# W3 product with features in partitions, its result turned by exchange and block turn, and one written list for the last two groups

## The chip, the cores and the metric

The kernel runs on one core of a Trainium2 chip. TensorE does the matmuls, VectorE and ScalarE move and combine what TensorE leaves in PSUM, GpSimd (POOL in the profile) does the small arithmetic of the norms and issues some DMAs, and SyncE (SP) issues the other DMAs. The metric is the time of one execution on the device in microseconds. The kernel before took 2526.16 us (median of 3 runs, 2524.74 to 2527.15).

## What is computed

The input x is [128, 128, 256] in fp32: 128 graphs of 128 nodes with 256 features; adj is one 128 x 128 matrix for all graphs. Four layers follow each other, and each adds its result to x after a layer norm and a relu. Cut to what matters here:

```
x += relu(gated messages along adj, along adj.T, and the node itself)   # layer 0
x += softmax(q k.T / 16, causal) v, then Wo                             # layer 1
x += A (relu(A (relu(A (h W1)) W2)) W3)     # layer 2: 256 -> 512 -> 1024 -> 256
x += BN(relu(BN(A_hat h W1.T)) W2.T)        # layer 3: 256 -> 512 -> 256
```

A mixes the nodes of one graph. The batch norms of layer 3 take mean and variance over all 16384 rows, so everything behind the first of them waits until all graphs have come to it. The change concerns the product by W3 in layer 2.

## The kernel before, in words

**Groups and streams.** The graphs are worked on in 32 groups of 4 (G), 512 tokens (T) each. The first pass brings every group through layers 0, 1 and 2 and through layer 3 up to its first product, which is stored as Z; it also stores x as X3. Between the passes the statistics of the first batch norm are closed (bn_affine, L1064), while 41 transposes keep TensorE running (awake, L1061). The second pass (L1151 on) normalizes Z, multiplies by the second matrix and keeps the statistics of the second batch norm; at the end the results are normalized, transposed and added to X3.

**Order of the work.** Each layer of a group is a Python generator that hands over after each small step. In turn g of the first pass (loop at L1041) four are in progress: A is layer 0 of group g+2, B layer 1 of group g+2 (its start belongs to the turn before, where it is called b), C layer 2 of group g, D layer 3 of group g-1 (its start, d, likewise). The string TURN (L983) says whose step is next, and in_turn (L88) pins the instructions of each step behind those of the step before on PE, VectorE, ScalarE, POOL and SP. So each engine's order is that of the list, and an instruction that waits holds up all that come later on its engine. HEAD (L1015) is the list for the start and group 0. The last turn, g = 31, follows FINAL (L992) by longer stages that are not pinned.

**Products.** `seven` (L524) multiplies two matrices as 2 x 2 blocks with seven block products: p_x, p_y, p_z are its PSUM tiles, `kept` (L529) copies one to SBUF on ScalarE (tiles ..._t), and `put` adds or copies to the result. Who is stationary and who moves is set by the product function. rows_by_half (L492) holds activations stationary, 128 tokens at a time, and streams 128 columns of weights (the matmul is at L499): the result has tokens in partitions. columns_by_half (L507) holds 128 columns of weights and streams 256 tokens (L516): the result has features in partitions. W2's product and layer 3's use the second form, W1's and W3's the first.

**Layer 2 before.** layer2 (L851) makes h2T, the 1024 features after W2, with features in partitions. The sums of its quarters are h2s. The third product multiplies h2s by the block combinations SETS["3"] of W3 with rows_by_half (L897), 7 x 8 matmuls of 128 columns per group, and put_s (L884) writes s with tokens in partitions: three additions on VectorE (L892) and one copy on ScalarE (L890), 128x256 each. Then pr = A s (L905, two matmuls of 512 columns; its stationary operand s must have tokens in partitions), VectorE adds pr to x (L907), and POOL stores x as X3 (L911). s shares its buffer, tag "qv", with layer 1's qv.

**Transposition by exchange.** Where other tiles have to be turned, the kernel uses swap and cut: swap (L439) stores a tile to DRAM with four DMAs (L444) and loads it back with one (L448), all on SP, so that blocks of 32 x 32 change their places; cut (L450) turns each block within itself with one VectorE transpose (L452). Layer 1 does this for h (DMAs hc, cut into hT, 128x1024) and for the attention weights (pc, cut into p, 128x512), layer 0 for the gate matrix (cc, cut into m). p's cut is what the attention product py (L794) waits for.

**Layer 3.** layer3 (L914) norms x, mixes it into gT (pg, L926, evicted at L466), makes its sums gs, and multiplies with columns_by_half (pz). VectorE and ScalarE bring pz to zo (L938, L946), bn_stats (L942, L952) records the statistics, and SP stores zo in two halves as Z (L957). bn_part (L973) aggregates the statistics with one bn_aggr for each of four feature chunks: "most1" for groups 0 to 29, ahead of the last turn in the program (L1045), "last1" for groups 30 and 31 after it (L1060). Names in the profile: mv_most and mv_last.

Of the kernel before, what the change touches and what calls it, by code (L numbers as in the profile page):

```python
# [15 lines left out]
P = 128  # L16
# [6 lines left out]
def kernel(  # L23
# [468 lines left out]
    def rows_by_half(a_r, b_r, wide):  # L492


        def product(r, pb, first):
            nk = a_r[r].shape[1]
            for rr in range(2):
                for c in range(nk):
                    nc.tensor.matmul(  # L499
                        pb[:, rr, :], a_r[r][:, c, rr * P : (rr + 1) * P], b_r[r][:, c, :wide],  # L500
                        start=(first and rr == 0 and c == 0), stop=(c == nk - 1),
                        skip_group_check=True,
                    )

        return product
# [344 lines left out]

    def layer2(g):  # L851

        xt, us = X[g], US[g]
        h2T = w.tile([P, HC2, T], FP, tag="h2T", name=f"h2T_{g}", bufs=1)

        a11, a12, a21, a22 = quarters_t(h2T)
        ex = w.tile([P, 3, HC2 // 2, T // 2], FP, tag="h2s", name=f"h2s_{g}", bufs=1)
        h2s = (a11, a12, ex[:, 2], a22, ex[:, 0], ex[:, 1], a21)

        def wide(q):  # L860
            def put(ij, pb, other):
                i, j = ij
                j = j * HC2 // 2 + 2 * q
                dst = h2T[:, j : j + 2, i * T // 2 : (i + 1) * T // 2]
                if other is None:
                    nc.scalar.activation(dst, pb, AF.Relu)
                    mine = slice(2 * q, 2 * q + 2)
                    yield SPLIT
                    yield from sums(
                        nc.vector,  # L870
                        [a[:, mine] for a in (a11, a12, a21, a22)], ex[:, :, mine],
                    )
                else:
                    nc.vector.tensor_tensor(dst, pb, other, ALU.add)  # L874
                    yield SPLIT
                    nc.scalar.activation(dst, dst, AF.Relu)  # L876

            return seven(
                columns_by_half(us, SETS["2"], 2 * q), put, [P, 2, T // 2], f"p2_{g}_{q}"
            )  # L880

        S = []

        def put_s(ij, pb, other):  # L884
            i, j = ij
            if not S:
                S.append(w.tile([P, G, D], FP, tag="qv", name=f"s_{g}", bufs=1))
            dst = S[0][:, 2 * i : 2 * i + 2, j * P : (j + 1) * P]
            if other is None:
                nc.scalar.copy(dst, pb)  # L890
            else:
                nc.vector.tensor_tensor(dst, pb, other, ALU.add)  # L892
            return ()

        yield from wide(0)
        late = wide(1)
        third = seven(rows_by_half(h2s, SETS["3"], P), put_s, [P, 2, P], f"p3_{g}")  # L897
        if g == LAST:
            for part in (late,) * 6 + (third,):
                yield from stage(part)  # L900
        yield from late
        yield from third
        for q in range(G // 2):
            pr = bank([P, 2, D], f"pr_{g}_{q}")
            nc.tensor.matmul(pr, a2T, S[0][:, 2 * q : 2 * q + 2, :], start=True, stop=True)  # L905
            yield SPLIT
            nc.vector.tensor_tensor(  # L907
                xt[:, 2 * q : 2 * q + 2, :], pr, xt[:, 2 * q : 2 * q + 2, :], ALU.add
            )
            yield SPLIT  # L910
        nc.gpsimd.dma_start(X3[g].rearrange("(b n) d -> n b d", n=P), xt)  # L911
        yield

    def layer3(g):  # L914


        parts = [ALL] if g < LAST else HALVES
        for bs in parts:
            relus = yield from norm(g, 3, bs)
            if g < LAST:  # L920
                yield
            h = yield from relus()
            yield
        gT = tile_of(g, parts[0], [P, DC, T], "dT", f"gT_{g}", 2)
        for i, bs in enumerate(parts):
            yield from mixed(gT, h, ahT, f"pg_{g}_{i}", (nc.vector.tensor_copy,), bs)  # L926
            if g < LAST:
                ex = w.tile([P, 3, 1, T // 2], FP, tag="ex", name=f"gs_{g}", bufs=2)
                gs = yield from sums(nc.vector, quarters_t(gT), ex)
            yield  # L930
        z = ZT[g] = [zp.tile([P, 2, T], FP, tag="z", name=f"zo_{g}_{j}") for j in range(2)]
        done = []

        def put(ij, pb, other):
            i, j = ij
            dst = z[j][:, :, i * T // 2 : (i + 1) * T // 2]
            if other is not None:
                nc.vector.tensor_tensor(dst, pb, other, ALU.add)  # L938
            if g >= LAST - 1:
                at = 2 * g - LAST + 1 + i  # L940
                for jj in range(2):
                    nc.vector.bn_stats(  # L942
                        stats1[:, 2 * j + jj, at, :], (pb if other is None else dst)[:, jj, :]
                    )
            if other is None:
                nc.scalar.copy(dst, pb)  # L946
            done.append(j)
            if done.count(j) == 2:
                if g < LAST - 1:
                    for jj in range(2):  # L950
                        yield SPLIT
                        nc.vector.bn_stats(stats1[:, 2 * j + jj, g, :], z[j][:, jj, :])  # L952

        if g < LAST:
            yield from seven(columns_by_half(gs, SETS["b"], 0), put, [P, 2, T // 2], f"pz_{g}")
            for j in (1, 0):
                nc.sync.dma_start(Z[g][:, 2 * j : 2 * j + 2, :], z[j])  # L957
            yield
            return
        for i, j in (0, 0), (1, 0), (0, 1), (1, 1):  # L960
            pb = bank([P, 2, T // 2], f"pz_{g}_{i}_{j}")
            for jj in range(2):
                for c in range(DC):
                    at = (2 * j + jj) * P
                    b = bw1T_12[:, jj * P : (jj + 1) * P] if (c, j) == (0, 1) else bw1T[:, c, at : at + P]
                    nc.tensor.matmul(
                        pb[:, jj, :], b, gT[:, c, i * T // 2 : (i + 1) * T // 2],
                        start=(jj == 0 and c == 0), stop=(c == DC - 1), skip_group_check=True,
                    )
            yield from put((i, j), pb, None)  # L970
            yield

    def bn_part(stats, nch, groups, name):  # L973

        mv = const.tile([P, nch, 2], FP, name=f"mv_{name}")
        for j in range(nch):
            nc.vector.bn_aggr(mv[:, j, :], stats[:, j, groups].rearrange("p g s -> p (g s)"))
        return mv[:, :, 0], mv[:, :, 1]
# [2 lines left out]


    TURN = (  # L983
        "DCDCCCCCBDBBBBBBBBABBBDDDAABBBBCCDDAAAABBDCCCBBCCBBACCAADDDDAADDAAACCDBA"
        "CCCCCCCCCCCCDDDABCCCCCCBBBADDBBBCCBBBBCCDCCACCCCCCAAAAABBbbbBBBBBDDBBBCC"
        "CCCbCCbBBBBBBBBBDDBBBBBBCDBDDBCCCdBBBBCCCdBBdBBBBBbB"
    )
    BEGUN = 6
    PINNED = tuple(
        getattr(mybir.EngineType, e) for e in ("PE", "DVE", "Activation", "Pool", "SP")  # L990
    )
    FINAL = "CCCCCCCCDCCCCCCCCCCDCCCCDDdDDddDdDdDDdddd"  # L992
    US = {}
    AHEAD = 3

    def stage(stream):

        for end in stream:
            if not end:
                yield  # L1000
                return
            yield end
# [6 lines left out]
    def part(f, g):  # L1009
# [8 lines left out]
        "dbbbeddbedfffoobbbbbbpppdopdbbbbbbbbdCfffffdddfAAffnCCfffffffffAddddfofp"  # L1018
        "ofoAddddndpAAfffddddddddfdffddCddfCCCCCCffnnACCCCfCoAACCAACCACCCCCCCCCCA"
        "AnnnnnAfCCCCCCoffffffAffffCCCCCCACCACCCCfffnCfAAAAABBBffffffffnCConBfBff"  # L1020
        "ffoofCCCfCffffooCCfffCCCCCDDDfffffffffffffB"
    )
    load_x(AHEAD)
    ds, bs = layer3(0), layer1(2)
# [13 lines left out]
        for _ in stream[k]:  # L1038
            pass
    assert len(nc.cur_bb.bb.instructions) == at  # L1040
    for g in range(1, NG):  # L1041
        if g + AHEAD < NG:
            load_x(g + AHEAD)
        if g == LAST:
            most1 = bn_part(stats1, FC, slice(LAST - 1), "most1")  # L1045
        stream = {
            "A": part(layer0, g + 2), "B": bs, "C": layer2(g), "D": ds,
            "b": part(layer1, g + 2), "d": layer3(g),
        }
        for k in TURN if g < LAST else ():  # L1050
            at = len(nc.cur_bb.bb.instructions)
            next(stream[k], None)
            in_turn(at, PINNED)
        for k in FINAL if g == LAST else ():
            step(stream[k])
        assert all(next(stream[k], k) == k for k in "ABCD")
        bs, ds = stream["b"], stream["d"]
    for _ in ds:
        pass
    last1 = bn_part(stats1, FC, slice(LAST - 1, NG + 2), "last1")  # L1060
    awake(41)  # L1061
    passA.close()

# [238 lines left out]
```

## Time and profile before

| | us |
|---|---|
| median of 3 runs | 2526.16 (2524.74 to 2527.15) |
| the profiled execution | 2523.98 |
| its span, first to last instruction | 2521.3 |
| PE busy | 2480.3 |
| VectorE busy | 1972.8 |
| ScalarE busy | 1181.2 |
| POOL busy | 309.3 |
| distance of two turns (the same piece of the chain: 286.83, 355.85, 424.87) | 69.02 |

A profile line of the groups reads: source line, engine, operation, written tile <- read tiles, sizes, count, then times in us or ns as its header says. The chain of waits lists the pieces of work that followed each other until the last instruction: start, duration, engine, tile, line, number of records. A DMA line gives the queue, the count, the size of one and the median time from issue to landing.

### The profile page before, as it was taken

How to read it: one execution, taken by the hardware profiler on the slowest of the kernel's cores; microseconds unless marked ns; L12 is line 12 of the kernel's file. 1: busy time of each engine (PE TensorE's matmuls, PEld its weight loads, DVE VectorE, ACT ScalarE, POOL GpSimd, SP SyncE). 2: the span in 40 equal slices, each digit the busy share in tenths (PEclk: the TensorE clock that was granted, in tenths of full speed). 3: DMA queues.
4: the chain of work that ended last, by engine and by line, in shares of the span. 5: the costliest groups of instructions: out<-in, count | busy, mean ns of one | idle time of the engine just before them, and what ended most of it. 6: DMA issues, size and time to landing. Idle time of an engine off the chain costs nothing.

```text
span 2521.3 us, 40758 instructions
## 1 busy us (share of the span) xinstructions
PE 2480.3 (98%) x14820; PEld 2243.0 (89%) x14820; DVE 1972.8 (78%) x4861; ACT 1181.2 (47%) x2486; POOL 309.3 (12%) x563
## 2 busy tenths in 40 slices
PE   8999999999999999999999999999999999999996
PEld 6899999999999999999999999999999999888875
DVE  7888777877777788777877777787778777558876
ACT  5444444444444444444444444444444444337766
POOL 2111111111111111111111111111111111000001
PEclk9999999999999999999999999999999999999998
DMA  3111222212222212222212222212222212135559
GB/s 137 55 43 55 66 68 67 67 59 61 68 67 60 59 43 59 68 68 68 63 59 65 67 59 59 54 50 65 68 68 64 58 55 59 34 132 201 180 188 391
DMA packets 115180, 206.54 MB, mean 82 GB/s; under 512 B 11538, under 2 KB 77092, under 8 KB 111012
## 3 DMA queue, kind: packets, MB, share of 16 engines
q1 hardware_dynamic: 108404, 180.80, 23.3%
q0 software_dynamic: 6432, 23.07, 2.6%
q8 instruction: 117, 1.92, 0.3%
q14 instruction: 83, 0.68, 0.1%
q10 hardware_dynamic: 144, 0.07, 0.0%
HBM read 105.20 MB, written 98.70 MB: 81 GB/s over the span
## 4 chain that ended last, share of the span: by engine, by line
PE 96%; ACT 2%; DVE 1%; issue 0%; DMA 0%; POOL 0%; ACTq 0%; DVEq 0%; POOLq 0%
PE p_x L516 18%; PE p_x L499 9%; PE p_z L516 9%; PE p_z L499 5%; PE pmu L462 5%; PE p_y L516 4%; PE po_x L1174 4%; PE pu_x L499 4%; PE pz_x L516 4%; PE pm L462 2%; PE ps L749 2%; PE p_y L499 2%; PE pg L462 2%; PE pm L658 2%; PE pr L905 2%; PE py L794 2%
## 5 line engine op out<-in xcount | busy, mean ns | idle before, releaser
L412 ACT ACTIVATE h<-x,sh,rs 128x256 f32<-128x256 f32 x512 | 266.5, 590 | 478.4 <-POOL sh L398 468.2
L516 PE MATMUL p_x<-uT,w 128*128 128x256 f32 x1024 | 242.1, 379 | 0.0
L876 ACT ACTIVATE h2T<-h2T 128x512 f32<-128x512 f32 x192 | 121.0, 630 | 257.9 <-DVE h2T L874 257.9
L516 PEld LDWEIGHTS p_x<-uT,w 128*128 128x128 f32 x1024 | 189.7, 190 | 23.4 <-ACT p_t L531 0.2
L395 POOL TENSOR_SCALAR rs<-mv 128x4 f32<-128x4 f32 x124 | 36.3, 293 | 1386.9 <-DVE mv L391 1384.9
L387 DVE BATCH_NORM_STATS2 st<-x 128x6 f32<-128x256 f32 x512 | 185.3, 414 | 3.1
L594 DVE SCALAR_TENSOR_TENSOR gs<-h,gw 128x256 f32<-128x256 f32 x360 | 152.4, 423 | 41.7 <-ACT h L412 30.2
L462 PEld LDWEIGHTS pmu<-a2T,u 128*128 128x128 f32 x1024 | 124.2, 192 | 29.2 <-issue 21.5
L531 ACT COPY p_t<-p_x 128x512 f32<-128x512 f32 (+1 forms) x192 | 97.5, 508 | 74.6 <-PE p_x L499 71.3
L396 POOL TENSOR_TENSOR rs<-rs,nhalf 128x4 f32<-128x4 f32 x124 | 129.7, 1046 | 10.3
L499 PE MATMUL p_x<-w,h2T 128*128 128x128 f32 x1024 | 124.7, 275 | 0.0
L462 PE MATMUL pmu<-a2T,u 128*128 128x128 f32 x1024 | 124.5, 275 | 0.0
L499 PEld LDWEIGHTS p_x<-w,h2T 128*128 128x128 f32 x1024 | 121.9, 192 | 1.7
L516 PE MATMUL p_x<-uT,set 128*128 128x256 f32 x512 | 121.2, 379 | 0.6 <-DVE h2T L874 0.6
L516 PE MATMUL p_x<-us,set 128*128 128x256 f32 x512 | 121.1, 379 | 0.0
L516 PE MATMUL p_z<-us,w 128*128 128x256 f32 x512 | 121.1, 379 | 0.0
L516 PE MATMUL p_y<-uT,w 128*128 128x256 f32 x512 | 121.0, 379 | 0.0
L516 PE MATMUL p_z<-us,set 128*128 128x256 f32 x512 | 120.9, 379 | 0.0
L874 DVE TENSOR_TENSOR h2T<-p_z,p_t 128x512 f32<-128x512 f32 x64 | 44.0, 687 | 87.2 <-PE p_z L516 87.2
L516 PEld LDWEIGHTS p_x<-uT,set 128*128 128x128 f32 x512 | 97.0, 190 | 14.1 <-DVE h2T L874 1.0
L516 PEld LDWEIGHTS p_y<-uT,w 128*128 128x128 f32 x512 | 97.2, 190 | 13.2
L516 PEld LDWEIGHTS p_z<-us,set 128*128 128x128 f32 x512 | 97.2, 190 | 13.2
(331 smaller groups left out, 5991.3 us busy)
## 6 DMA issues: line engine op xcount, KB each, us to landing
z<-zo SPq DMA_DIRECT2D x62, 512.0 KB, 5.1
zi<-z SPq DMA_DIRECT2D x31, 1024.0 KB, 4.8
x<-x POOLq DMA_DIRECT2D x32, 512.0 KB, 3.5
x<-in_x_dram SPq DMA_DIRECT2D x31, 512.0 KB, 3.9
hc<-h SPq DMA_DIRECT2D x120, 128.0 KB, 2.5
h<-hc SPq DMA_DIRECT2D x30, 512.0 KB, 4.2
out_dram<-x3i SPq DMA_DIRECT2D x30, 512.0 KB, 10.7
x3i<-x SPq DMA_DIRECT2D x20, 512.0 KB, 6.7
```

Source lines behind the costliest of these rows:

```text
L387: nc.vector.bn_stats(st[:, k, :], xt[:, b, :])
L396: nc.gpsimd.tensor_tensor(rs, rs, nhalf[:, :n], ALU.pow)
L412: nc.scalar.activation(dst, src, AF.Relu, bias=sh[:, k : k + 1], scale=rs[:, k : k + 1])
L462: nc.tensor.matmul(pm[:, k, :], src[:, b, c * P : (c + 1) * P], aT, start=True, stop=True)
L499: nc.tensor.matmul(pb[:, rr, :], a_r[r][:, c, rr * P : (rr + 1) * P], b_r[r][:, c, :wide], start=(first and rr == 0 and c == 0), stop=(c = ...
L516: nc.tensor.matmul(pb[:, jj, :], b_r[r][:, c, at : at + P], a_r[r][:, c, :], start=(first and jj == 0 and c == 0), stop=(c == nk - 1), ski ...
L531: nc.scalar.copy(t, pb)
L594: nc.vector.scalar_tensor_tensor(gs, h[:, b, :], 1.0, gw[:, i, :], ALU.mult, ALU.mult, accum_out=gl[:, k, i : i + 1],)
L658: nc.tensor.matmul(pm[:, r, :], cmbT[:, b, :], h[:, b, :], start=True, stop=True)
L749: nc.tensor.matmul(ps[:, k, :], qv[:, b // 2, c, 0, (b % 2) * P : (b % 2 + 1) * P], hT[:, c, b * P : (b + 1) * P], start=(c == 0), stop=(c ...
L876: nc.scalar.activation(dst, dst, AF.Relu)
L1174: nc.tensor.matmul(pb, BW2R[r][:, c, :], a_r[r][:, c, :], start=(first and c == 0), stop=(c == FC // 2 - 1), skip_group_check=True,)
```

## The change

For the groups 1 to 30 ("crossed") the third product holds W3's blocks stationary and streams 256 tokens (product_s), 7 x 4 matmuls per group. put_s writes its result in pieces of 32 columns into one half of a buffer twice as long as s (the buffer's slot, shared with qv, had that length already). At the end of layer2, swap sends this half through DRAM (five DMAs on SP, named sc). At the start of layer3 of the same group, which lies in the next turn, cut turns it into the other half (VectorE, 128x1024), and mixed_last, taken out of layer2, does pr, the addition to x and the store of x. Groups 0 and 31 keep rows_by_half and do mixed_last in place for themselves.

TURN is a new list for the turns 1 to 29, with 8 instead of 6 steps of b begun ahead; HEAD gets two more steps of B; layer 3 of group 0 gets 8 empty steps ahead. The last two groups follow one list, TAIL, whose steps are all pinned: B, C, D go on, E is layer 2 of group 31, F and G layer 3 of groups 30 and 31, and S makes most1 and last1 at fixed places.

```diff
--- before.py
+++ after.py
@@ -850,7 +850,7 @@
 
     def layer2(g):
 
-        xt, us = X[g], US[g]
+        us = US[g]
         h2T = w.tile([P, HC2, T], FP, tag="h2T", name=f"h2T_{g}", bufs=1)
 
         a11, a12, a21, a22 = quarters_t(h2T)
@@ -880,29 +880,55 @@
             )
 
         S = []
+        crossed = 0 < g < LAST
 
         def put_s(ij, pb, other):
             i, j = ij
             if not S:
-                S.append(w.tile([P, G, D], FP, tag="qv", name=f"s_{g}", bufs=1))
-            dst = S[0][:, 2 * i : 2 * i + 2, j * P : (j + 1) * P]
+                S.append(w.tile([P, 2, G, D], FP, tag="qv", name=f"s_{g}", bufs=1))
+            if crossed:
+                dst = S[0][:, 0].rearrange("p b d -> p (b d)").rearrange(
+                    "p (t b k r) -> p k b t r", t=NQ, b=G, k=DC
+                )[:, j, 2 * i : 2 * i + 2]
+                pb, other = (
+                    a and a.rearrange("p (b t r) -> p b t r", b=2, t=NQ) for a in (pb, other)
+                )
+            else:
+                dst = S[0][:, 1, 2 * i : 2 * i + 2, j * P : (j + 1) * P]
             if other is None:
                 nc.scalar.copy(dst, pb)
             else:
                 nc.vector.tensor_tensor(dst, pb, other, ALU.add)
             return ()
 
+        def product_s(r, pb, first):
+            for c in range(HC2 // 2):
+                nc.tensor.matmul(
+                    pb, SETS["3"][r][:, c, :], h2s[r][:, c, :],
+                    start=(first and c == 0), stop=(c == HC2 // 2 - 1), skip_group_check=True,
+                )
+
         yield from wide(0)
-        late = wide(1)
-        third = seven(rows_by_half(h2s, SETS["3"], P), put_s, [P, 2, P], f"p3_{g}")
-        if g == LAST:
-            for part in (late,) * 6 + (third,):
-                yield from stage(part)
-        yield from late
+        if crossed:
+            third = seven(product_s, put_s, [P, T // 2], f"p3_{g}")
+        else:
+            third = seven(rows_by_half(h2s, SETS["3"], P), put_s, [P, 2, P], f"p3_{g}")
+        yield from wide(1)
         yield from third
+        if crossed:
+            across = S[0][:, 0].rearrange("p b d -> p (b d)")
+            swap(across, f"sc_{g}")
+            MIX[g] = S[0]
+            yield
+            return
+        yield from mixed_last(g, S[0][:, 1])
+
+    def mixed_last(g, s):
+
+        xt = X[g]
         for q in range(G // 2):
             pr = bank([P, 2, D], f"pr_{g}_{q}")
-            nc.tensor.matmul(pr, a2T, S[0][:, 2 * q : 2 * q + 2, :], start=True, stop=True)
+            nc.tensor.matmul(pr, a2T, s[:, 2 * q : 2 * q + 2, :], start=True, stop=True)
             yield SPLIT
             nc.vector.tensor_tensor(
                 xt[:, 2 * q : 2 * q + 2, :], pr, xt[:, 2 * q : 2 * q + 2, :], ALU.add
@@ -914,6 +940,11 @@
     def layer3(g):
 
 
+        if g in MIX:
+            s = MIX.pop(g).rearrange("p k b d -> p k (b d)")
+            cut(s[:, 1], s[:, 0], DC * G)
+            yield
+            yield from mixed_last(g, s[:, 1].rearrange("p (b d) -> p b d", b=G))
         parts = [ALL] if g < LAST else HALVES
         for bs in parts:
             relus = yield from norm(g, 3, bs)
@@ -981,16 +1012,21 @@
 
 
     TURN = (
-        "DCDCCCCCBDBBBBBBBBABBBDDDAABBBBCCDDAAAABBDCCCBBCCBBACCAADDDDAADDAAACCDBA"
-        "CCCCCCCCCCCCDDDABCCCCCCBBBADDBBBCCBBBBCCDCCACCCCCCAAAAABBbbbBBBBBDDBBBCC"
-        "CCCbCCbBBBBBBBBBDDBBBBBBCDBDDBCCCdBBBBCCCdBBdBBBBBbB"
+        "ACCCBCCCCCAADBDBBBCDDCDDCCDDABBBBBAADCCBBCBCDBBAADABDCBBABBCCCCCCAAACCCD"
+        "CCCAADDDDAADCDDCCCDBBCCAADBBCDBBBBBBBBCCCCAAAAADDDBBbCCCCCCCbbBBBBBCCbbB"
+        "BDDBBDBBBBBBBBCCBCCBBBCCCCBBBDBDDDDDDDBBBBBBBBbBBBBdbb"
     )
-    BEGUN = 6
+    BEGUN = 8
     PINNED = tuple(
         getattr(mybir.EngineType, e) for e in ("PE", "DVE", "Activation", "Pool", "SP")
     )
-    FINAL = "CCCCCCCCDCCCCCCCCCCDCCCCDDdDDddDdDdDDdddd"
-    US = {}
+    TAIL = (
+        "CCCCCCCBBBDDDDDDBBBBBBBDDCDCCBBBCCBCCDBBBBBDCCCCCBCCCCCCCCCBCCBCCCCCCBBB"
+        "DBBCCBBBBBCCCBCCCCCCBCCCBBBCCCBBBBBBBBBBBBBDDCBBDBBBBBCCBDDDDBBBBBBCBBBB"
+        "BBBEEEEEEEEDDDDEFEEEEEEFFFEEEEEDDEEEEEEEEEEEEEEEDDDDDDDEEEEEEEFEEEEEEEFF"
+        "EFFDDDDEEEFEFFFFSFFFEEEFFEEEEFFFGGGDFFFFFGFFFFGGGGGGGGGFFFGGGGGS"
+    )
+    US, MIX = {}, {}
     AHEAD = 3
 
     def stage(stream):
@@ -1018,7 +1054,7 @@
         "dbbbeddbedfffoobbbbbbpppdopdbbbbbbbbdCfffffdddfAAffnCCfffffffffAddddfofp"
         "ofoAddddndpAAfffddddddddfdffddCddfCCCCCCffnnACCCCfCoAACCAACCACCCCCCCCCCA"
         "AnnnnnAfCCCCCCoffffffAffffCCCCCCACCACCCCfffnCfAAAAABBBffffffffnCConBfBff"
-        "ffoofCCCfCffffooCCfffCCCCCDDDfffffffffffffB"
+        "ffoofCCCfCffffooCCfffCCCCCDDDfffffffffffffBBB"
     )
     load_x(AHEAD)
     ds, bs = layer3(0), layer1(2)
@@ -1038,26 +1074,49 @@
         for _ in stream[k]:
             pass
     assert len(nc.cur_bb.bb.instructions) == at
-    for g in range(1, NG):
+
+    def after(n, stream):
+
+        for _ in range(n):
+            yield SPLIT
+        yield from stream
+
+    ds = after(8, ds)
+    for g in range(1, LAST - 1):
         if g + AHEAD < NG:
             load_x(g + AHEAD)
-        if g == LAST:
-            most1 = bn_part(stats1, FC, slice(LAST - 1), "most1")
         stream = {
-            "A": part(layer0, g + 2), "B": bs, "C": layer2(g), "D": ds,
+            "A": layer0(g + 2), "B": bs, "C": layer2(g), "D": ds,
             "b": part(layer1, g + 2), "d": layer3(g),
         }
-        for k in TURN if g < LAST else ():
+        for k in TURN:
             at = len(nc.cur_bb.bb.instructions)
             next(stream[k], None)
             in_turn(at, PINNED)
-        for k in FINAL if g == LAST else ():
-            step(stream[k])
         assert all(next(stream[k], k) == k for k in "ABCD")
         bs, ds = stream["b"], stream["d"]
-    for _ in ds:
-        pass
-    last1 = bn_part(stats1, FC, slice(LAST - 1, NG + 2), "last1")
+    def statistics():
+
+        nonlocal most1, last1
+        most1 = bn_part(stats1, FC, slice(LAST - 1), "most1")
+        yield
+        last1 = bn_part(stats1, FC, slice(LAST - 1, NG + 2), "last1")
+        yield
+
+    most1 = last1 = None
+    stream = {
+        "B": bs, "C": layer2(LAST - 1), "D": ds, "E": layer2(LAST), "F": layer3(LAST - 1),
+        "G": layer3(LAST), "S": statistics(),
+    }
+    for k in TAIL:
+        at = len(nc.cur_bb.bb.instructions)
+        next(stream[k], None)
+        in_turn(at, PINNED)
+    at = len(nc.cur_bb.bb.instructions)
+    for k in stream:
+        for _ in stream[k]:
+            pass
+    assert len(nc.cur_bb.bb.instructions) == at
     awake(41)
     passA.close()
```

## The prediction

> **What bounds the kernel.** I read four views in this order: the shares and the chain, the chain's pieces in one turn, engine time by stretch, and the groups of the operations that move. First the page.
>
> ```profile
> span 2521.3 us, 40758 instructions
> PE 2480.3 (98%) x14820; PEld 2243.0 (89%) x14820; DVE 1972.8 (78%) x4861; ACT 1181.2 (47%) x2486; POOL 309.3 (12%) x563
> PE 96%; ACT 2%; DVE 1%; issue 0%; DMA 0%; POOL 0%; ACTq 0%; DVEq 0%; POOLq 0%
> ```
>
> TensorE is busy 98% of the span and is 96% of the chain that ended last. So the time is TensorE's own work plus 40 us, most of which lies at the start, at the step into the second pass and in the final output. The chain inside one turn:
>
> ```profile
> 857.11 1.78 PE p_x L499 x16
> 858.90 1.79 PE p_y L499 x16
> 860.68 1.79 PE p_z L499 x16
> ...
> 908.00 3.45 PE p_x L516 x16
> ```
>
> The pieces abut: 857.11 + 1.79 = 858.90. Each fp32 matmul is two records. A record of 128 moving columns (L499, the W3 product) takes 1.79 / 16 = 111.7 ns, one of 256 columns (L516) 3.45 / 16 = 215.7 ns. Then two whole turns (columns: stretch, then busy us of PE, PEld, DVE, ACT, POOL, the granted clock, DMA share, GB/s):
>
> ```profile
> 860.00:929.00 69.00, 69.00 (x425) 62.93 (x424) 54.94 (x140) 30.92 (x67) 9.35 (x18) 1.00 0.22 62
> 929.00:998.00 69.00, 69.00 (x424) 62.93 (x423) 54.94 (x140) 30.92 (x67) 9.35 (x18) 1.00 0.22 62
> ```
>
> A turn costs 69.0 us, all of it TensorE, at full clock. VectorE has 14 us free in it. So a TensorE saving in a turn counts in full, as long as no other engine becomes late for TensorE.
>
> **What the Trainium skill says.** "TensorE: Matmul & The Clock Gate", section "Wait — 56ns, not 53.3ns?": a warm matmul costs its columns at 2.4 GHz plus a fixed 2.5 ns or so. The same columns in fewer, wider matmuls save only that fixed part. The trace agrees: two records of 128 cost 223.3 ns against 215.7, 7.6 ns less. The same page, "Architectural detail: the array is 16× 32×32, not 1× 128×128": VectorE and ScalarE take their queue strictly in order. So a late instruction holds all behind it; the trace has no VectorE record out of program order in the turn I listed. "DMA: Bandwidth & Descriptors", "Issuing engines are not separate DMA queues": transfers from all queues share the same engines. The trace bears on it: the Z store landed in 2.6 to 7.5 us though its size is fixed.
>
> **The change, part by part.** The sum is made against the profiled execution, 2523.98 us (span 2521.3). The median of the runs shown, 2526.16, lies 2.2 above.
>
> *W3 product.* Removed per group: 56 matmuls of 128 columns, 112 records x 111.65 ns = 12.50 us. Added: 28 of 256 columns, 56 x 215.8 = 12.08. Saved 0.42 us, in 30 groups (1 to 30): 12.4 us. The moving operand is now the activations and the stationary one the weights; the columns streamed are the same, which is why the gain is so small. Lower bound 0 (if swapped operands brought a new load wait), upper 12.8; the L516 rows already run this form without idle time, so I take 12.4.
>
> *put_s in 32-column pieces.* Same sizes, four per group. VectorE's add of 128x256 took 415 ns and ScalarE's copy 366. ScalarE's relu (L412) already writes both plainly and in such pieces, and its 512 records lie between 583 and 605 ns, so the pieces cost 0 to 0.02 us. I take 0.
>
> *The exchange.* Added per group: five SP DMAs (four stores of 128 KB, one load of 512 KB), one VectorE block turn, one turn of delay for pr, the addition to x and the POOL store of x. The nearest rows are those of layer 1's exchange, same sizes:
>
> ```profile
> h<-hc SPq DMA_DIRECT2D x30, 512.0 KB, 4.2
> hc<-h SPq DMA_DIRECT2D x120, 128.0 KB, 2.5
> z<-zo SPq DMA_DIRECT2D x62, 512.0 KB, 5.1
> L452 DVE STREAM_TRANSPOSE hT<-h x30: 1235/1236/1239, 129.9 to 2130.9; 128x1024 f32<-128x1024 f32 x30
> ```
>
> In a turn of before, hc's first issue was at 872.14, its fifth at 875.96: 3.8 us, then 4.2 to landing, 8.0 together. Counting time from a turn's first p_x (nominal length now 68.6), the last s copy ends at 63.9; the exchange lands at 71.9, 3.3 us into the next turn. VectorE reaches the cut at about 4.8, behind hT's cut and the sums of uT, and ends it at 6.0. TensorE wants pr at 6.9. So VectorE has 0.9 us of margin, the landing 1.5 us before VectorE arrives and about 2 in all. Cost 0. If the cover is gone, every us of lateness is paid 30 times. On SP, hc's five issues end at 57, before sc's; behind sc stand the two Z stores (a few us later, nobody waits soon), the x load (used a turn later), pc and cc (pc is wanted at about 26). On POOL the store of x moves with its step; the norm chains there need 9.35 us per turn, and the issue stands ahead of none that is urgent.
>
> *VectorE's queue in the new list.* The added cut raises VectorE from 54.9 to 56.2 us of 68.6, but the new order also packs it. From 17.6 us to the first py (35.58), its instructions are: qv copy 0.60; nine gate sums at 0.467 start to start, 4.20; gT copy 0.60; mask and maximum 1.31; four sums of h2T 2.75; gate add and reciprocal 0.44; a wait for ScalarE's first scaled copy 0.47; eight gate matrices 2.60 and an addition 0.60; gT copy 0.60; three sums 1.25; two biases 0.79; sum and addition 0.96; reciprocal and p's cut 0.80. That is 17.97, so p is ready at 35.6. In before the cut ended 3.9 us ahead of py:
>
> ```profile
> L452 DVE STREAM_TRANSPOSE p<-pT x1: 706/706/706, 917.0 to 917.0; 128x512 f32<-128x512 f32 x1
> ...
> L794 PE MATMUL py<-qv,p x8: 379/379/379, 921.7 to 924.0; 128*128 128x256 f32 x8
> ```
>
> Adding 17 durations leaves an error of 0.3 or so; stall 0 to 0.4 us. I take 0.1, in 29 turns 3 us (0 to 12). All other margins that I find are 0.4 us or more, but for one of 0.1 (an addition into h2s ahead of p_x at 61.5), which I count in the same range.
>
> *The last two groups.* The records of the four aggregations of 30 groups (all six of such size):
>
> ```profile
> L977 DVE BATCH_NORM_AGGREGATE mv_most<-stats x6: 908/966/989, 2178.5 to 2449.8; 128x2 f32<-128x180 f32 x4, 128x2 f32<-128x186 f32 x2
> ```
>
> In before the four lay free in VectorE's idle time from 2178.5 on. The new list puts them between the two gT copies of group 30, at about 44 us into the last group; they take 4 x 0.9 to 0.97, 3.6 to 3.9 us. Behind them wait the second gT copy, the sums of gT, both additions of pr, the norm of group 31 and ScalarE's relus. TensorE wants pz_z at 50.5 and gets its operand at about 54.6: 4.1 us, with small ones after it 4.9. Before's own end of the pass had 1.9 us of such stalls, so net 3.0 (0, if other matmuls fill more than I found, to 5). All four short aggregations now follow the last statistic, 2 x 0.22 more on the path to the second pass, hidden in part by the 41 transposes of awake: 0.3. The second pass is the same: 0.
>
> Sum: -12.4 + 3 + 3.0 + 0.3 = -6.1. 2523.98 - 6.1 = 2517.9 on the profiled execution, 2526.16 - 6.1 = **2520.0** on the median. Groups 0 and 31 keep the old product, and turn 1 only runs eight empty steps more: 0, within 1 us.
>
> **Rivals.**
> (a) Everything hidden: py's cut is in time and the tail costs no more than before's. -12.4 gives 2513.8. For it: every turn of before ran without a stall. Against it: the packed 18 us on VectorE, and 3.6 us of aggregations in front of work that TensorE needs.
> (b) The gain is spent: 0.3 us at py in 29 turns (8.7) and 5 at the tail: +1.3, 2527.5. For it: py has no reserve in my sum, and any forgotten dependent wait (30 ns each) adds to it.
> (c) Slower: the exchange is late. Place: the cut of s at the head of VectorE's queue in each turn. It waits for a landing, and VectorE's additions and the TensorE order stand behind it. Price: 30 times the excess. It decides from a last landing of 6.2 us instead of 4.2 (2.0 of margin); net slower once the excess passes 0.4 us. A Z store of equal size took up to 7.5, that is 1.3 over: 30 x 1.3 = 39, 2559. Against it: the Z stores are issued behind sc's load, and the load of hc with the same neighbours behind it stayed at 4.2.
> (d) That the change does not do what it says is excluded for TensorE: fewer, wider matmuls stand in its order. Its price difference of 7.6 ns per pair comes from this trace.
>
> **How the numbers follow.** Chances: forecast 0.42, (a) 0.26, (b) 0.20, (c) 0.12. The measurement can tell about 0.2%, 5 us: faster means under 2521.1, slower over 2531.2. The forecast's own range is 2516 to 2524, three quarters of it faster: 0.31, with (a) 0.57; a tenth goes to no change from the forecast, and most of (b), 0.17: 0.28; slower is (c) and a part of (b): 0.15. Range: from 2512 (a) with the upper bound of the product, to 2531 (the end of (b): stall 0.4, tail 5), which leaves (c) and little else out.
>
> **What would show it.** The W3 rows should be 28 matmuls x 2 records a group of about 216 ns pitch; a turn should be 68.6 us plus the stall, read as the distance of the same piece in two turns. A stall ahead of py, put down to VectorE's cut, shows the third step; a stall ahead of pr, put down to DMA or the cut of s, shows (c); a gap of some 4 us ahead of pz_z of group 30 behind mv_most shows the tail. The prediction is wrong if the turn is longer than 69.0, if sc's load lands over 6 us after its issue, or if the pitch of the new records is not that of L516.

## The result, and the profile after

The changed kernel takes 2521.2 us (median of 20 runs, 2519.43 to 2523.46), the one before 2524.88 in the 20 runs that now stand for it. The ratio is 0.9985, 95% interval 0.9978 to 0.9992: 3.7 us faster. The forecast was 2520.0 with a range from 2512 to 2531, 6.1 us faster; in the measured 20 runs 6.1 us less would have been 2518.8.

The page of the changed kernel, the lines that answer to those shown of before:

```profile
span 2519.4 us, 37791 instructions
PE 2474.5 (98%) x13140; PEld 2187.2 (87%) x13140; DVE 2006.5 (80%) x4891; ACT 1163.2 (46%) x2486; POOL 315.0 (13%) x563
PE 88%; issue 8%; DMA 1%; DVE 1%; ACT 1%; POOL 0%; SPq 0%; DVEq 0%; POOLq 0%; ACTq 0%
```

TensorE has 14820 - 13140 = 1680 records fewer, 30 groups x 56, as the change says. VectorE is busy 34 us longer: the 30 block turns of 1.24 us are 37, and all its other work together takes 3 less. The 8% called issue in the chain is no loss: nearly all of it is one piece of 200.13 us from 2252.89 on, the second pass, for which the chain names no work, and TensorE is busy for 198 us of it. Now one turn, from the start of ps in group 13 to that in group 14 (columns: stretch, busy us of PE, PEld, DVE, ACT, POOL, granted clock, DMA share, GB/s):

```profile
903.43:972.16 68.73, 68.73 (x368) 60.99 (x367) 56.06 (x141) 30.28 (x68) 9.59 (x17) 1.00 0.27 78
```

The stretch is 68.73 us long where before had 69.02. The saving is 0.29 us, not the 0.42 that the product's records give. The busy share shows nothing of the other 0.13: TensorE is busy for all of the 68.73 us. The ends of its records are modelled, so small gaps don't show there. The chain can tell (start, duration, engine, tile, line, records):

```profile
849.63 1.00 PE py L794 x4
...
918.37 1.00 PE py L794 x4
...
920.23 0.86 PE py L794 x4
```

The first py of each turn takes 1.00 us for four records, the second 0.86. In before both took 0.86:

```profile
852.80 0.86 PE py L794 x4
...
854.52 0.86 PE py L794 x4
```

In the records it is a gap of 60 ns ahead of the first py and a stretched distance of 75 ns behind it. The list of waits does not show so small a gap; the two pieces side by side do.

**Where the time went.** I put against each other, for both profiled executions, the start times of TensorE's records, and took off what their columns cost at full clock (111.65, 215.8 and 429.8 ns for a record of 128, 256 and 512). What is left over is called lost time (us):

| stretch | before | after | difference |
|---|---|---|---|
| columns of all records | 2453.7 | 2441.1 | -12.6 |
| lost, from the start to layer 2 of group 0 | 16.9 | 19.0 | +2.0 |
| lost, turn 1 | 0.0 | 0.5 | +0.5 |
| lost, turns 2 to 29 | 0.2 | 4.0 | +3.7 |
| lost, groups 30 and 31 to the end of the pass | 1.9 | 6.4 | +4.5 |
| lost, between and behind the passes (and group 0) | 25.4 | 25.7 | +0.3 |

The sum is -1.6 us, and the spans differ by 1.9 (2521.3 and 2519.4); the other 0.3 lies ahead of TensorE's first record and behind its last. I do not count the start-up row as an effect of the change: its code and its order are the same, and in the profiled executions of all the kernels below layer 2 of group 0 begins between 54.7 and 57.7 us with no relation that I can see to what they change (57.2 in E9, which keeps the old lists, 54.7 in E2, which has the new ones). For one thing, TensorE's wait for a loaded weight matrix is 1.0 us there in this execution and is missing in that of E2. Without this row the sum is -3.6, and the medians say -3.7.

**The end of the pass.** The two longest waits of TensorE in the last groups (columns: sum us, times, longest):

```profile
PE pz_z L516 <- ACT pz_t L531: 3.6, 1, 3.6
...
PE p_x L906 <- ACT p_t L531: 0.6, 1, 0.6
```

The chain of the changed kernel from 2226 us on shows who made the first of them late:

```profile
2225.99 3.35 DVE mv_most L1008 x4
2229.34 0.54 DVE gT L466
...
2231.60 1.20 DVE x L933 x2
...
2234.10 0.74 POOL rs L224
...
2235.57 0.59 ACT h L412
2236.16 0.47 ACT pz_t L531
2236.63 0.04 issue
2236.68 1.13 PE pz_z L516 x4
2237.81 1.42 PE pz_x L516 x4
2239.22 2.88 PE pg L462 x16
```

Read upwards from pz_z: it waits for ScalarE's copy pz_t, this stands behind group 31's relu (h), the relu waits for POOL's and VectorE's norm, and VectorE comes to that norm only after the additions, the gT copy and the four aggregations of 30 groups, 3.35 us. The two last lines show a second loss: 16 records of 128 columns (pg) take 2.88 us instead of 1.79. The stretches around it:

```profile
2226.00:2232.00 6.00, 6.00 (x34) 4.75 (x33) 5.93 (x11) 0.96 (x2) 0.00 (x0) 1.00 0.00 0
2232.00:2236.50 4.50, 1.11 (x6) 0.63 (x4) 3.44 (x12) 1.44 (x3) 1.57 (x2) 1.00 0.34 117
2236.50:2239.00 2.50, 2.32 (x8) 1.95 (x9) 1.59 (x7) 1.11 (x3) 0.70 (x1) 0.80 0.02 7
2239.00:2242.00 3.00, 3.00 (x18) 2.98 (x17) 2.93 (x9) 0.59 (x2) 0.00 (x0) 0.60 0.25 98
2242.00:2248.00 6.00, 6.00 (x30) 5.28 (x30) 2.87 (x8) 1.76 (x3) 0.00 (x0) 1.00 0.58 186
```

After a gap of 3.73 us the granted clock falls to 0.80 and 0.60 on average in these stretches. TensorE starts again at 2236.7 at full clock; from 2238.0 to 2241.4 its records come at twice their distance (427 instead of 216 ns, 213 instead of 112), 1.6 us together. The profiled executions of E1, E5, E6 and E7 have the same gap and a half clock behind it too. The Trainium skill describes this ("TensorE: Matmul & The Clock Gate", section "What's actually happening"): a window of about 3.4 us, which runs freely, without work halves the clock until a busy window has passed. This trace agrees in length (3.41 us) and in factor. It does not agree in "without work": the last section shows that a window need not be wholly idle.

### The profile page after: what moved, and what is told of

It is laid out like the page before. It is cut to its first block, busy times and chain, and to the rows that moved or that the text cites. A ratio compares the mean times of both kernels' runs of the same rounds, so it can differ in the third digit from the quotient of the medians.

```text
span 2519.4 us, 37791 instructions
## 1 busy us (share of the span) xinstructions
PE 2474.5 (98%) x13140; PEld 2187.2 (87%) x13140; DVE 2006.5 (80%) x4891; ACT 1163.2 (46%) x2486; POOL 315.0 (13%) x563
## 4 chain that ended last, share of the span: by engine, by line
PE 88%; issue 8%; DMA 1%; DVE 1%; ACT 1%; POOL 0%; SPq 0%; DVEq 0%; POOLq 0%; ACTq 0%
PE p_x L516 18%; PE p_z L516 9%; PE p_x L906 8%; PE pmu L462 5%; PE p_y L516 4%; PE pu_x L499 4%; PE pz_x L516 4%; PE p_z L906 4%; PE pm L462 2%; PE py L794 2%; PE ps L749 2%; PE pg L462 2%; PE pm L658 2%; PE pqv_x L704 2%; PE pu_z L499 2%
## 5 line engine op out<-in xcount | busy, mean ns | idle before, releaser
L396 POOL TENSOR_TENSOR rs<-rs,nhalf 128x4 f32<-128x4 f32 x124 | 142.4, 1149 | 10.3
L516 PEld LDWEIGHTS p_z<-us,w 128*128 128x128 f32 x512 | 97.2, 190 | 25.4 <-issue 6.9
L825 ACT ACTIVATE u<-u 128x512 f32<-128x512 f32 x93 | 58.7, 631 | 125.2 <-DVE u L823 125.2
L983 DVE BATCH_NORM_STATS2 stats<-zo 128x6 f32<-128x512 f32 x120 | 77.2, 685 | 46.1 <-ACT zo L977 45.1
L906 PE MATMUL p_x<-h2T,w 128*128 128x256 f32 x480 | 113.4, 379 | 0.0
L516 PEld LDWEIGHTS p_x<-us,set 128*128 128x128 f32 x512 | 97.2, 190 | 13.2
```

What stands on the lines that cost most here:

```text
L396: nc.gpsimd.tensor_tensor(rs, rs, nhalf[:, :n], ALU.pow)
L516: nc.tensor.matmul(pb[:, jj, :], b_r[r][:, c, at : at + P], a_r[r][:, c, :], start=(first and jj == 0 and c == 0), stop=(c == nk - 1), ski ...
L906: nc.tensor.matmul(pb, SETS["3"][r][:, c, :], h2s[r][:, c, :], start=(first and c == 0), stop=(c == HC2 // 2 - 1), skip_group_check=True,)
```

## The experiments

The theory: the product saves its 12.6 us in full; 3.7 come back at py, because VectorE's packed queue is late with p, and 4.5 at the end, because of the aggregations and the half clock behind them. The exchange itself is hidden. Rivals: the new products or the added transfers make the turn longer by themselves; ScalarE's order makes the gap at the end.

**E1, p's cut one addition earlier.** In the second line of TURN (at its 17th letter):

```diff
-        "CCCAADDDDAADCDDCCCDBBCCAADBBCDBBBBBBBBCCCCAAAAADDDBBbCCCCCCCbbBBBBBCCbbB"
+        "CCCAADDDDAADCDDCBBCCDCCAADBBCDBBBBBBBBCCCCAAAAADDDBBbCCCCCCCbbBBBBBCCbbB"
```

CCDBB became BBCCD: B's reciprocal and cut go ahead of C's addition and relu. Nothing else is changed.

> In the turns 1 to 29 VectorE's reciprocal and block turn of the attention weights go ahead of one addition into h2T instead of behind it; nothing else changes. Theory (VectorE's queue is late for py): the 0.135 us gap ahead of py goes, the turn falls from 68.73 to 68.60, 3.8 us in 28 turns, time 0.9970 of before instead of 0.9985. Rival (the new products or the extra DMA traffic make the turn 0.13 longer than the columns give, and py only shows it): the gap turns up elsewhere and the turn stays at 68.73.

Measured: 2518.19 us, ratio 0.9972 (0.9962 to 0.9982). The chain of this run:

```profile
916.16 0.86 PE py L794 x4
917.88 0.86 PE py L794 x4
984.75 0.86 PE py L794 x4
986.48 0.86 PE py L794 x4
```

Both py take 0.86 us, and the turn is 984.75 - 916.16 = 68.59 us. The gap is gone: lost time in the turns 2 to 29 fell from 4.0 to 1.0 us. Of this, 0.8 is in two turns alone, at the mixing product pm, and open; the other turns have no gap in its place. So VectorE's order made it. That neither the transfers nor the width of the product does is shown by E6 and E5, which leave the gap as it is.

**E2, the long aggregations late.** Each of the four got its own place between the last products of group 31, where VectorE waited 0.96 us for TensorE:

```diff
-        most1 = bn_part(stats1, FC, slice(LAST - 1), "most1")
-        yield
+        mv = const.tile([P, FC, 2], FP, name="mv_most1")
+        for j in range(FC):
+            nc.vector.bn_aggr(
+                mv[:, j, :], stats1[:, j, slice(LAST - 1)].rearrange("p g s -> p (g s)")
+            )
+            yield
+        most1 = mv[:, :, 0], mv[:, :, 1]
...
-        "EFFDDDDEEEFEFFFFSFFFEEEFFEEEEFFFGGGDFFFFFGFFFFGGGGGGGGGFFFGGGGGS"
+        "EFFDDDDEEEFEFFFFFFFEEEFFEEEEFFFGGGDFFFFFGFFFFGGGGGGGGGFFFGSGSGSGSGS"
```

> The four aggregations of 30 groups are taken out of VectorE's queue between the two gT copies of group 30 and put singly into its waits of 0.96 us in the last products. Theory (they make VectorE 3.35 us late, and TensorE pays for it): the 3.73 us gap ahead of pz_z of group 30 falls to 0.2 to 0.6, time 3.2 to 3.5 us below the changed kernel, 0.9971 of before. Rival (ScalarE's order, the relus of group 31 ahead of the pz copy, makes the gap by itself): 1.8 us of it or more stays.

Measured: 2517.52 us, 0.9971 (0.9959 to 0.9982), 3.7 below the changed kernel. TensorE's wait in this run:

```profile
PE pz_z L516 <- ACT pz_t L531: 1.2, 1, 1.2
```

The gap fell from 3.73 to 1.33 us, by 2.4 and not by the 3.1 to 3.5 expected. The time came out right by luck, because the half clock, which the expectation did not count, went too: the lost time from group 31's layer 2 to the end of the pass fell from 5.5 to 2.0. So two thirds of the gap were the aggregations. The last third is what the rival blamed on ScalarE's order, though less than the 1.8 it asked for; E4 tests it.

**E3, the edits of E1 and E2 together.**

> Both edits of the two runs before. Theory: they add, 7.1 us below the changed kernel, about 2514, 0.9957 of before; only the stalls of turn 1 (0.5 us) and some 3 us at the end are left of what was lost. Rival: one gap takes the place of the other and less than 4 us is gained.

Measured: 2513.71 us, 0.9956 (0.9943 to 0.9968). That is 7.5 below the changed kernel, 11.2 below the kernel before. The two losses add, and this is a version faster than both kernels.

**E4, both, and group 31's norm behind group 30's copies.** On top of E3, in TAIL (only the part of its last line that differs from E3 is shown):

```diff
-...FFFGGGDFFFFFGFFFFG...
+...FFFGDFFFFFGGGFFFFG...
```

> As the run with both edits, and the norm and relus of group 31's first half are put behind group 30's two pz copies on ScalarE. Theory: what e2 leaves of the gap at pz_z (0.2 to 0.6 us) goes, but pg of group 31 may then wait for its relus: between 0.5 us faster and 0.5 us slower than with both edits. Rival (ScalarE's order makes the gap): over 1.5 us faster than with both edits.

Measured: 2513.9 us, 0.9961 (0.9947 to 0.9974), not to be told from E3. The wait at pz_z is gone, and this stands in its place:

```profile
PE pg L462 <- ACT h L412: 0.9, 2, 0.7
```

Group 31's pg now waits for the relus that were moved. So ScalarE's order did make the rest of the gap, and removing it there only moves it: lost time in this stretch is 2.55 us against 2.01 in E3.

**E5, the product in 128 columns again.**

```diff
-                nc.tensor.matmul(
-                    pb, SETS["3"][r][:, c, :], h2s[r][:, c, :],
+                for e in range(2):
+                    of = slice(e * P, (e + 1) * P)
+                    nc.tensor.matmul(
+                        pb[:, of], SETS["3"][r][:, c, :], h2s[r][:, c, of],
...
```

> The changed kernel with each of product_s's matmuls split into two of 128 tokens: same weights held, same sums, 56 matmuls of 128 columns per crossed group again. Theory (the product's saving is only the fixed part per record): 30 x 0.42 = 12.6 us come back, about 2533.8, 1.0035 of before; the turn goes from 68.73 to 69.15 with the gap ahead of py unchanged. Rival (part of the saving comes from holding weights instead of activations): less than 9 us comes back.

Measured: 2533.72 us, 1.0036 (1.0022 to 1.0049), 12.5 above the changed kernel. The turn is 69.15, 0.42 longer, with the gap at py unchanged. The saving is the cost per record alone; it does not matter which operand is held. It is also what the exchange and the new lists would cost if the product saved nothing: 9 us slower than before.

**E6, no exchange.**

```diff
-            swap(across, f"sc_{g}")
...
-            cut(s[:, 1], s[:, 0], DC * G)
             yield
-            yield from mixed_last(g, s[:, 1].rearrange("p (b d) -> p b d", b=G))
+            yield from mixed_last(g, s[:, 0].rearrange("p (b d) -> p b d", b=G))
```

> The changed kernel without the exchange and the block turn of s: swap and cut of s are left out and the product pr reads s as it is, so that layer 2's result is not the reference's in groups 1 to 30. Theory (both are hidden): turn 68.73 and the gap of 0.13 ahead of py as before, time within 1.5 us of 2521. Rival (the added 1.24 us on VectorE or the added transfers make py late): the turn falls to 68.60, about 2517.

Measured: 2521.96 us, 0.9989 (0.9982 to 0.9996), no different from the changed kernel. The turn is 68.73, and the 0.13 at py stays. So the five transfers and the block turn cost nothing in their place. VectorE has emptied its queue before the packed stretch begins: in both runs it waits some 0.2 us for ScalarE's h, 19 us ahead of py. At the end of the pass this run loses 1.2 us more, with the same gap of 3.73: its half clock lasts 6.83 us instead of 3.41, since the gap begins at another point of the clock's window:

```profile
2236.50:2239.00 2.50, 2.50 (x7) 1.96 (x8) 1.20 (x6) 1.12 (x3) 0.70 (x1) 0.50 0.03 7
2239.00:2242.00 3.00, 3.00 (x14) 2.82 (x13) 2.76 (x8) 0.16 (x1) 0.00 (x0) 0.50 0.14 56
```

**E7, the exchange later.** Eight more stores go ahead of it on SP:

```diff
+            more = scratch.tile([8, P // 4, G * D], FP, name=f"more_{g}")
+            for k in range(8):
+                nc.sync.dma_start(more[k], across[k % 4 * 32 : k % 4 * 32 + 32])
             swap(across, f"sc_{g}")
```

> Eight more stores of 128 KB of s to DRAM go ahead of the exchange on SP, which nobody reads: the exchange starts about 8 x 0.44 = 3.5 us later. Theory (it has 1.4 us until VectorE comes to its cut and 1.05 from there to pr, 2.4 together): pr waits about 1.1 us in each of 30 turns, 25 to 40 us more, about 2553. Rival (SP's later loads or VectorE's queue break first): over 60 us; or the margin is larger than I read: under 10 us.

Measured: 2597.43 us, 1.0291 (1.0274 to 1.0309), 76 us above the changed kernel, where I had expected 25 to 40.

```profile
PE pr L934 <- DVE s L452: 58.1, 29, 3.7
```

The place is right: pr waits for the cut of s, in 29 turns, and the list of waits has nothing else new. The size was wrong. In a typical turn the load of s was issued 4.0 us later than in the changed kernel, not 3.5, and pr then waited 1.9: the margin is 2.1 us. The same difference gives 1.9 to 2.3 us in 21 of the 29 turns, but 0.6 to 1.8 in eight. In seven of these the changed kernel itself issues the load 4.4 to 5.3 us after the last copy of s instead of 3.8 to 4.1; why is open. By the records' starts the gaps ahead of pr add up to 62.8 us of the 74.7 by which the span grew. 9.4 more are records at half clock, which sets in in five places where the changed kernel has none, and 2.1 the late records behind the waits. This is the mechanism of rival (c), measured: once its margin is used up it would have made the change slower by far.

**E8 and E9, the old lists with the new product.** In the kernel before, only product_s and put_s were changed; s is not turned. In E8 put_s writes the pieces of 32 columns, in E9 the old places. The lines that differ (minus E8, plus E9):

```diff
-                dst = S[0].rearrange("p b d -> p (b d)").rearrange(
-                    "p (t b k r) -> p k b t r", t=NQ, b=G, k=DC
-                )[:, j, 2 * i : 2 * i + 2]
-                pb, other = (
-                    a and a.rearrange("p (b t r) -> p b t r", b=2, t=NQ) for a in (pb, other)
-                )
+                pb, other = (
+                    a and a.rearrange("p (b n) -> p b n", b=2) for a in (pb, other)
+                )
```

> The kernel before, its lists untouched, with only the W3 product of groups 1 to 30 in the new form; s is not turned, so that layer 2's result is not the reference's in those groups. Theory (the product saves by itself, whatever the list): turn 69.02 - 0.42 = 68.60, about 2512.4, 0.9950 of before, the end of the first pass as before. Rival (some wait of VectorE or ScalarE in the old list takes part of it back): 2515 to 2522.

> The kernel before, its lists untouched, with the W3 product of groups 1 to 30 in the new form, and its four results put where the old ones went, so that the first pr needs only the first two of them as before. s is not turned: layer 2's result is not the reference's in those groups. Theory (in the run with the old list and pieces of 32 columns the first pr waited for the last of the four results, 1.2 us per turn, and the product itself does save 0.42): no gap ahead of pr, turn 68.60, about 2512.4, 0.9950 of before. Rival (the old list loses time with the new product for another reason): the turn is 68.8 or more.

Measured: E8 2547.44 us, 1.0091 (1.0076 to 1.0106); E9 2511.57 us, 0.9947 (0.9933 to 0.9960). My expectation of E8 missed by 35 us. Its waits:

```profile
PE pr L924 <- ACT s L899: 29.0, 31, 1.0
```

With the pieces of 32 columns each half of s holds parts of all four results, so that the first pr needs the last of them, ScalarE's copy, 1.1 us after TensorE would have begun it, in a turn that became 69.82 us long. E9 takes that one dependency away, and the turn is 68.60: the product saves its 0.42 us in a list that was not made for it, with no other wait. E8 also shows that with the pieces of 32 columns pr could not stay at its old place for free, even without the exchange.

## Why the prediction was right, and where it was off

**Product: right.** Expected -12.4, measured -12.6 in the records, and 12.5 to bring back (E5). The 0.2 is a slip in the sum: its own 0.42 x 30 is 12.6. One reading beside it was too kind. The prediction says that the trace agrees with the Trainium skill ("TensorE: Matmul & The Clock Gate", section "Wait — 56ns, not 53.3ns?"), but a fixed 2.5 ns per matmul does not give the 7.6 ns of a pair: an fp32 record of 128 columns took 111.65 ns and one of 256 took 215.8, so a column costs about twice what 2.4 GHz gives, and the fixed part is 2 x 111.65 - 215.8 = 7.5 ns by these two sizes. The term is right because it was priced from the trace.

**Pieces of 32 columns: right.** VectorE's addition into s has a median of 425 ns instead of 414 to 418, ScalarE's copy 373 instead of 366. TensorE does not see it: the turn is 68.60 with the pieces (E1) and without them (E9).

**Exchange: right.** Expected cost 0 with about 2 us to spare at pr; E6 shows 0, E7 a margin of 2.1 in most turns and 0.6 in the tightest. The lines behind it, of the changed kernel:

```profile
sc<-s SPq DMA_DIRECT2D x120, 128.0 KB, 2.5
s<-sc SPq DMA_DIRECT2D x30, 512.0 KB, 4.1
...
L452 DVE STREAM_TRANSPOSE s<-s x30: 1233/1239/1246, 199.9 to 2191.1; 128x1024 f32<-128x1024 f32 x30
```

They are the rows of layer 1's exchange (2.5, 4.2 and 1.236) once more, as assumed.

**py: right in place, and near in size.** Expected 0.1 us in 29 turns, 3 us; measured 0.135, 3.7 us in 28 turns and 0.13 of turn 1's 0.5. The sum itself left p 0.02 us late, with an error of 0.3, so that such a near hit in size is in part luck; and only 0.06 of the 0.135 is the wait, the rest is the late record behind it, which the sum did not have. The stretch of VectorE's queue was added up to 17.97 us from rows of before; in the trace p's cut starts at 917.44 and lasts 0.68, and py begins 0.15 behind it.

**The last two groups: right in mechanism, too small in size.** The step that failed is "4.1 us, with small ones after it 4.9", net 3.0. The gap is 3.73, a little below the 4.1. But I let TensorE go on at full clock after it. The half clock that followed costs 1.6 us, which brings the net to 4.5. I also gave the aggregations nearly the whole gap; E2 gives them 2.4 us of it, and E4 puts the rest down to ScalarE's order.

**Turn 1: 0 within 1 us**, measured 0.5: the py gap of 0.13, and a gap of 0.35 at p_z in front of the first block sums.

Together the terms missed by 2.4 us of 6.1, 1.6 of them the half clock.

**Rivals.** (a) is nearly what E1 and E2 make of the kernel: E3 is 11.2 us below the kernel before, where (a) has 12.4. That 2513.7 and 2513.8 stand so close is chance, since the prediction counts from a median 1.2 us higher. (b) would have asked for 0.3 us at py. (c) did not happen; E7 shows its margin. (d) is excluded by E5 and E9.

## What to carry to other kernels

Wider matmuls with the same columns save only the cost per record, here 7.6 ns in 223; they pay only if everything that they bring in is hidden, so find the margin of each part in the queue of the engine that does it. When one engine is full, its list is a timetable for the others: add up the durations of the second engine's queue from a point where it is surely idle, and the place of a stall can be foreseen, its size only as well as the sum's error (here 0.3 us). Put long, unhurried instructions where that engine waits for the bound one, never ahead of what the bound one needs.

## What was not expected of the hardware

A gap of 3.73 us on TensorE cost 5.3, since 1.3 us behind it the clock halved for 3.4 us; the same gap in E6, begun at another time, cost 1.2 more, and one of 1.33 us (E2, E3) cost nothing beyond itself and one stretched record. In each trace the changes of the clock lie on a grid of 3.41 us. I laid the records, with what their columns cost, over this grid in all eleven traces, from 40 us on. Every window at full clock in which TensorE was idle for 65% or more was followed by one at half clock, 32 in all; no window with 58% or less was. The gap of 3.73 us falls on two windows of the changed kernel, 48% and 65% idle. In E6 the first was 82% idle, and the next, at half clock and 32% idle, was followed by another at half clock. The 1.33 us of E2 lie in a window that is 42% idle. So what such a gap costs depends on where it falls on the grid.

A record behind even a short wait comes about 0.1 us later than its columns say (75 ns behind py's gap of 60, 104 behind the longer ones), so that py's wait of 60 ns costs 135.
